# Measures, loads, residuals and spare steps of a two-layer attention and scan kernel put at other places in a hand-written order

## The chip, the cores and the metric

The kernel runs on one core of one Trainium2 chip. The metric is device time in microseconds (us). Three runs of the kernel before took 2679.15 to 2679.93 us, with a median of 2679.76.

## The reference

Two layers work on an image batch x of 2 × 56 × 56 tokens with 384 channels, in f32. Layer 0 is a neighborhood attention with 12 heads of 32 channels, in which each token sees 7 × 7 neighbors around it, and an MLP. Layer 1 is a projection, a depthwise convolution, four scans, and an MLP. Cut to what is computed:

```python
# layer 0
h   = layernorm(x) * ln1_g + ln1_b
q, k, v = split(h @ w_qkv + b_qkv)          # 12 heads of 32; q scaled by 32 ** -0.5
s   = q . k over the 7 x 7 neighbors + rpb  # window clipped at the edges
x   = x + (softmax(s) @ v) @ w_proj + b_proj
y   = layernorm(x) * ln2_g + ln2_b
x   = x + gelu(y @ w1 + b1) @ w2 + b2       # 384 -> 1536 -> 384
# layer 1
p     = (layernorm(x) * n1_g + n1_b) @ w_in + b_in      # 384 -> 768
local = depthwise_conv_3x3(p, k_conv)
scan(z): y[t] = 0.6 * y[t-1] + 0.4 * z[t]   # along rows and columns, both ways
mixed = 0.25 * (lr + rl + tb + bt) + local
x     = x + (layernorm(mixed) * on_g + on_b) @ w_out + b_out
x     = x + gelu((layernorm(x) * n2_g + n2_b) @ w1 + b1) @ w2 + b2
```

(The last line is the same MLP as in layer 0, with layer 1's own weights.)

## The kernel before

The order in which every engine works is written out by hand: the program is built under a manual schedule, and each engine takes its instructions in the order in which the Python code issues them. There are five engines: PE (matmuls and transposes), DVE (vector work), ACT (activations and scaling), POOL (a few small operations) and SP (whose queue issues the DMAs).

**Attention.** The 6272 tokens are cut into 14 groups n of 448 tokens (8 rows of 56; NG = 7 groups per image). A group has four windows of 112 query tokens, and the heads come in three head groups hg. So a group takes 12 steps, k = 0 to 11, and the whole loop has NU = 168 steps s = 12n + k and four more to drain. `Unit` is the work of one step, `Window` that of three steps. A step issues

- on PE the scores `sc` (L515) of step s, the values `o` (L556) of step s − 2, the sums of exponentials (L563), and one or two **fillers**: items of the list `ahead` (queries or keys, L386, and values, of later groups), a projection (L582) of a finished group, or transposes (L357) of the normalized tokens of group n + 3;
- on DVE `pts` (L530, scores plus bias), small steps of the softmax (`sum` L546 and L548, `turned` L482, `rec` L488, `good` L492, `rec_t` L498, `og` L500), the residual addition after a projection (`xr`, L590), and the statistics of the layer norm of group n + 3, one token tile at a time (`measure_x`, which issues the statistics L214 and L215; behind the last tile come `rs` L219, a power on POOL L222, and `sh` L233);
- on ACT the exponential of `pts` (L536), the normalization of `xg` (L240, `normalize_x`) and the copies out of PSUM;
- on POOL the softmax totals (L484, L494), and the addition of a bias to a residual tile (`add_bias`, L576), four steps after that tile was asked for.

SP's queue takes stores (L642) at the start of a step, then residual loads (L571, `load_residual`), group loads of `xg` (L302), bias loads (L316), and the vt load of a window (L465, values back from DRAM, in which `v_d` holds them). `ahead` has 9 items in odd groups and 10 in even ones. The tuple `spare` lists the steps k that take no item of `ahead`. In groups 0 to 11 these are (3, 4, 5) in odd groups and (4, 6) in even ones. Projections of the group before are issued from k = 3 on. From END = 12 on (the last two groups) there is little left in `ahead`, and projections go to the steps in THEN.

During the last 16 steps of the loop the two weights of layer 0's MLP are loaded in six parts (`w_parts`, L625), and behind the last step the first groups of the next stage (`xs`, tag "xa", L609) and four residual tiles.

```python
        if s < NU and hg == 2 and s + 1 < NU:
            ws[i + 1] = Window(i + 1)
        if s >= NU - UG - 4 and hg == 2 and w_parts:
            w_parts.pop(0)()
```

**The passes.** Layer 0's MLP and layer 1's projection `w_in` follow, over groups of token tiles (128 tokens each; up to four tiles a group). Then layer 0's MLP goes on beside the convolution and the scans of layer 1 (`Beside`, with the jobs `Band` and `Columns`, mostly on DVE): these are issued between PE's groups as their due times come, and `beside.until(...)` issues them up to a named job. `Columns` number NI = 6 jobs per image, one for every 128 channels, and store the mixed result to `mix_d` (L1259).

**The last stage** goes over the groups again: `load_mix` (L1274) loads a group's `mx` from `mix_d`, `measure` turns its tiles by PE (`xi`, L1288) and takes their statistics, `project_out` multiplies by `w_out`, and the MLP follows (`hid` L1080 and L1089, `y` L1096, out store L1526). `measure_beside` puts the measures of the next group between the twelve hidden columns m of the MLP of this group. The group `half_way` is the first that reaches into the second image, so it needs the last of that image's `Columns`; it is loaded tile by tile, 128 tokens of all channels at a time:

```python
            if g + 2 == half_way:
                beside.until((1, NI - 1))
                ahead = load_mix(g + 2)
```

Groups after `half_way` turn their tiles on DVE (L1299, `measure_by_vector`). The last DVE row, L1556, is the addition behind the last token tile.

Of the kernel before, what the change touches and what calls it, by code (L numbers as in the profile page):

```python
# [41 lines left out]
NH, KS, HD = 12, 7, 32  # L42
# [131 lines left out]
def block_kernel(ctx: ExitStack, tc: tile.TileContext, ins: dict, out: bass.AP):  # L174
# [467 lines left out]
            nc.sync.dma_start(out=dst, in_=src)  # L642


    tps = [any_bank() for c in range(NC)]
    halves = [Norm(sm) for h in range(2)]
    for h, norm in enumerate(halves):
# [39 lines left out]
        channels_of(2, c, any_bank)()  # L687
    load_bias(0, 3)
    for t in range(3):
        load_residual(t)  # L690
    shift_by_values(ep, ps_t, wproj, shift)
    sctx.close()

# [13 lines left out]
    for s in range(NU + 4):  # L707
        n, k, hg, i = s // UG, s % UG, s % NC, s // NC
        if s == NU:

            kctx.close()
            xp = ctx.enter_context(tc.tile_pool(name="x", bufs=2, side="right", reuse_waits="tile"))
            tail_pool = actx.enter_context(tc.tile_pool(name="a_tail", bufs=1))
            xs = {g: load_group(x1f, groups[g], "xa") for g in range(2)}
            for t in range(T2 // P - 4, T2 // P):
                load_residual(t, tail_pool, 4, 2)
        store_all()
        while load:
            load_residual(load.pop(0))
        if k == 0 and n < ng:  # L720
            vals = []
            if n + 1 < ng:
                ahead += [lambda n=n, m=m: query_or_key(n + 1, m, one_bank) for m in range(NC)]
                vals += tiles_of(n + 1)[2:]
            if n + 2 < ng:
                vals += tiles_of(n + 2)[:2]
            ahead += [lambda t=t: value(t, one_bank) for t in vals]
            if n + 2 < ng:
                ahead += [
                    lambda n=n, m=m: query_or_key(n + 2, m, one_bank) for m in range(NC, 2 * NC)  # L730
                ]

            spare = (3, 4, 5) if len(ahead) == 9 else (4, 6)

        if k == 2 and n + 4 < ng:
            load_x(n + 4)
        if k == 1 and n < ng:
            load_bias(n, NWC - 1)
        if n + 1 < ng and k in (4, 10):
            load_bias(n + 1, 0 if k == 4 else 1)  # L740
        if s == NU - UG - 4:
            ectx.close()
            wm = ctx.enter_context(tc.tile_pool(name="w_mlp", bufs=1, side="right"))
            w1, w2, w_parts = weights(0)
        if s < NU and hg == 2 and s + 1 < NU:
            ws[i + 1] = Window(i + 1)
        if s >= NU - UG - 4 and hg == 2 and w_parts:
            w_parts.pop(0)()

        if s <= NU:  # L750
            for take in taking:
                take()
            taking = []
        if s == NU + 1:
            sctx.close()
            ps_s = sctx.enter_context(tc.tile_pool(name="a_pss", bufs=4, space=PSUM))
        if s < NU:

            if s not in units:
                units[s] = Unit(ws[i], hg)  # L760
                units[s].scores()
                behind = Unit(ws[(s + 1) // NC], (s + 1) % NC) if s + 1 < NU else None
                if behind is not None and (units[s].m + behind.m) * TT <= BANK:
                    behind.scores(units[s].m)
                    units[s + 1] = behind
        new, before, last = units.get(s), units.get(s - 1), units.pop(s - 2, None)
        done = last.w if last is not None and last.hg == NC - 1 else None
        if last is not None:
            last.values()
        behind = ws.get(i - 1 - (hg == 0))  # L770
        if behind is not None and hg == 2:
            behind.invert()
        if behind is not None and hg == 0:
            behind.divide()
            if behind.j == NWC - 1:
                to_project += tiles_of(behind.n)
            ws.pop(behind.i)
        if n + 3 < ng and k < NT:
            measure_x(n + 3, k)
        for half in range(2):  # L780
            if new is not None:
                new.biased(half)
                new.numerators(half)
            if half == 0 and done is not None:
                done.take()
        if before is not None:
            before.gathered()
        if done is not None:
            done.gather()
        if n < END:  # L790
            if ahead and k not in spare:
                taking.append(ahead.pop(0)())
            if to_project and n < END - 1:
                taking.append(project(to_project.pop(0), turning_bank))
        elif ahead:
            if k != 3:
                taking.append(ahead.pop(0)())
        elif s - END * UG in THEN:
            taking.append(project(to_project.pop(0), one_bank))
        elif s > NU and s < NU + 4 and to_project:  # L800
            taking.append(project(to_project.pop(0), any_bank))
        for t in list(loaded):
            loaded[t] -= 1
            if loaded[t] < 0:
                add_bias(t)
        if n + 3 < ng:
            if k in (4, 5):
                for q in range(2 * k - 8, 2 * k - 6):
                    normalize_x(n + 3, q)
            if k in (8, 9, 11):  # L810
                taking.append(channels_of(n + 3, (8, 9, 11).index(k), turning_bank))
# [159 lines left out]
    def passes(xs, xn, w1, w2, between=lambda ps: None):  # L971
# [294 lines left out]
        def load_mix(g):  # L1266
            t0, n = dgroups[g]
            mx = io.tile([P, NI, MT], F32, name="mx")

            step = P if g == half_way else n * P  # L1270
            for t in range(0, n * P, step):
                for b, at, here, size in images(t0 + t, step):
                    here += t
                    nc.sync.dma_start(  # L1274
                        out=mx[:, :, here : here + size],
                        in_=mix_d[b][:, :, at : at + size].rearrange("m p t -> p m t"),
                    )
            x = load_group(x2_d, dgroups[g], "xa")
            if g >= half_way:
                add_row(x, dgroups[g][1], "b_out")  # L1280
            return mx, x, Norm(sm)
# [23 lines left out]
        def measure_beside(m, g, ahead):  # L1305


            n = dgroups[g][1]
            if g > half_way:
                if m % 2 == 0 and m // 2 < n:  # L1310
                    measure_by_vector(ahead[0], ahead[2], m // 2)
            elif m % 2 == 1 and 0 < m // 2 <= n:
                measure(ahead[0], ahead[2], m // 2 - 1)
            if m == 10:
                ahead[2].close(n)

        def project_out(g, mx, x, inner):
# [174 lines left out]
        for g, (t0, n) in enumerate(dgroups):  # L1492
# [37 lines left out]
                    add_row(x3, dgroups[g + 1][1], "b2_1")  # L1530
                beside.go(ROW_D)
            if g + 2 == half_way:
                beside.until((1, NI - 1))
                ahead = load_mix(g + 2)
        pctx.close()

# [90 lines left out]
```

## Time and profile before

| what | value |
|---|---|
| median of 3 runs | 2679.76 us (2679.15 to 2679.93) |
| profiled execution, own time | 2680.04 us |
| its span | 2678.2 us |
| PE busy | 2640.3 us (99%), 14963 instructions |
| DVE busy | 1963.2 us (73%), 3539 instructions |
| ACT busy | 898.7 us (34%) |
| POOL busy | 249.7 us (9%) |
| DMA | 298.99 MB moved, mean 112 GB/s |
| granted clock of PE, mean | 0.996 of full |

The span is the time from the first to the last recorded instruction; the execution's own time is the device time of that same run, 1.8 us more. Busy time is the time in which an engine has an instruction at work; PE's weight loads are counted on their own and lie beside its matmuls. The clock is what the throttle granted to PE: 1.00 is full rate and 0.50 half. The views used below are the table of waits (for every instruction and what released it: total us, times, longest), the windows (for a stretch of time: its length, the busy time of every engine, and the clock) and the timeline (instructions in order of time: start, duration, engine, line, operation, output and inputs).

### The profile page before, as it was taken

What the parts mean: (1) busy time and instruction counts of PE and PEld (TensorE: products, weight loads), DVE (VectorE), ACT (ScalarE), POOL (GpSimd) and SP (SyncE); (2) the same over time, 40 slices, a digit from 0 to 9 for tenths busy, and PEclk for the clock granted to TensorE, in tenths of its full rate; (3) what the DMA queues carried; (4) which work ended last, traced back from release to release, by engine and by line L of the source; (5) the groups of instructions that cost most, each with busy time, mean ns of one, the idle gap of its engine ahead of it and who ended that gap; (6) DMA issues with size and microseconds to landing.
All of it is one profiled execution on the core that took longest, in us unless ns stands there. A gap on an engine that the chain in (4) does not pass through costs nothing. (4 is left out here: it accounts for less than half of the span.)

```text
span 2678.2 us, 37275 instructions
## 1 busy us (share of the span) xinstructions
PE 2640.3 (99%) x14963; PEld 1473.9 (55%) x14963; DVE 1963.2 (73%) x3539; ACT 898.7 (34%) x1447; POOL 249.7 (9%) x264
## 2 busy tenths in 40 slices
PE   8999999999899999999999999999999899999999
PEld 4666666656655455555555555555555455555556
DVE  3778877876365698688989889888988627677652
ACT  4555555554322332223344422311143211111111
POOL 1111111111211100000010000000010011101100
PEclk9999999999999999999999999999999999999999
DMA  6323454224411132233346544533346401111000
GB/s 216 134 89 102 154 170 146 80 77 158 156 37 38 65 107 88 89 128 105 123 156 230 184 149 150 178 120 114 118 182 228 152 19 37 45 44 39 30 12 17
DMA packets 134249, 298.99 MB, mean 112 GB/s; under 512 B 11463, under 2 KB 89905, under 8 KB 131761
## 3 DMA queue, kind: packets, MB, share of 16 engines
q1 hardware_dynamic: 134064, 296.50, 32.3%
q8 instruction: 119, 1.95, 0.3%
q14 instruction: 66, 0.53, 0.1%
HBM read 180.86 MB, written 115.61 MB: 111 GB/s over the span
## 5 line engine op out<-in xcount | busy, mean ns | idle before, releaser
L1080 PE MATMUL mm<-hT,w 128*128 128x512 f32 (+2 forms) x1872 | 771.1, 569 | 0.4 <-ACT hT L254 0.2
L1080 PEld LDWEIGHTS mm<-hT,w 128*128 128x128 f32 x1872 | 352.7, 190 | 383.5 <-issue 352.1
L1089 ACT ACTIVATE hid<-mm,chan 128x512 f32<-128x512 f32 (+2 forms) x312 | 206.1, 661 | 683.3 <-PE mm L1080 683.2
L1096 PE MATMUL y_end<-w,hid 128*128 128x384 f32 x1200 | 395.2, 486 | 0.0
L1174 DVE SCALAR_TENSOR_TENSOR loc<-pt,taps,loc 128x990 f32<-128x990 f32 (+9 forms) x336 | 377.1, 1122 | 10.0 <-ACT loc L1156 1.7
L1096 PE MATMUL y<-w,hid 128*128 128x384 f32 x1152 | 379.4, 486 | 0.0
L1096 PEld LDWEIGHTS y_end<-w,hid 128*128 128x128 f32 x1200 | 227.5, 190 | 157.2
L1096 PEld LDWEIGHTS y<-w,hid 128*128 128x128 f32 x1152 | 218.2, 190 | 150.5 <-issue 1.0
L530 DVE TENSOR_TENSOR pts<-sc,bias 119x448 f32<-119x448 f32 (+3 forms) x336 | 220.9, 699 | 78.2 <-PE sc L515 75.2
L536 ACT ACTIVATE pts<-pts 119x448 f32<-119x448 f32 (+3 forms) x336 | 206.8, 642 | 191.3 <-DVE pts L530 187.9
L222 POOL TENSOR_TENSOR rs<-rs,mhalf 128x4 f32<-128x4 f32 (+4 forms) x67 | 87.1, 1300 | 1727.0 <-DVE rs L219 1691.6
L386 PE MATMUL ps<-hT,wqkv 128*128 128x448 f32 x504 | 212.0, 559 | 2.0 <-ACT qT L396 0.7
L1064 DVE STREAM_TRANSPOSE hT<-xn 32x96 f32<-32x96 f32 x672 | 181.1, 269 | 31.4 <-PE mm L1080 11.8
L1080 PE MATMUL mm<-hT,w_in 128*128 128x512 f32 (+2 forms) x468 | 191.9, 568 | 0.6 <-ACT hT L254 0.6
L240 ACT ACTIVATE xn<-xc,sh,rs 128x384 f32<-128x384 f32 x98 | 64.7, 698 | 268.6 <-DVE sh L233 268.5
L1080 PEld LDWEIGHTS mm<-hT,w_in 128*128 128x128 f32 x468 | 88.5, 190 | 102.1 <-issue 90.6
L386 PEld LDWEIGHTS ps<-hT,wqkv 128*128 128x128 f32 x504 | 90.2, 191 | 82.8 <-issue 73.1
L515 PEld LDWEIGHTS sc<-qT,kT 32*100 32x100 f32 (+3 forms) x3168 | 91.6, 170 | 67.1 <-issue 17.9
L1299 DVE STREAM_TRANSPOSE turned<-mx 32x192 f32<-32x192 f32 x336 | 123.3, 367 | 4.2
L515 PE MATMUL sc<-qT,kT 32*100 32x112 f32 (+3 forms) x3168 | 114.7, 272 | 6.5 <-DVE pts L530 5.8
L556 PE MATMUL o<-pts,vt 100*32 100x112 f32 (+3 forms) x3168 | 112.7, 266 | 3.8 <-DMA vt<-v_d 2.7
L582 PE MATMUL ps<-wproj,og 128*128 128x384 f32 x294 | 107.1, 503 | 3.6 <-DVE xr L590 3.6
(104 smaller groups left out, 2644.9 us busy)
## 6 DMA issues: line engine op xcount, KB each, us to landing
bias<-in_bias_t SPq DMA_DIRECT2D x16, 1344.0 KB
loc<-loc_d SPq DMA_DIRECT2D x24, 784.0 KB
mixed<-mix_d SPq DMA_DIRECT2D x24, 784.0 KB
mix_d<-mixed SPq DMA_DIRECT2D x24, 784.0 KB
xa<-x_d SPq DMA_DIRECT2D x22, 768.0 KB
p_d<-mx SPq DMA_DIRECT2D x10, 1536.0 KB
mx<-mix_d SPq DMA_DIRECT2D x10, 1536.0 KB
pt<-p_d SPq DMA_DIRECT2D x18, 560.0 KB
```

The costliest lines, as they stand in the source:

```text
L386: nc.tensor.matmul(ps, lhsT=wqkv[:, c, m * P : (m + 1) * P], rhs=hT[:, c, half_of(n)], start=c == 0, stop=c == NC - 1,)
L515: nc.tensor.matmul(sc[i // 2][: w.keys, i % 2, (first + c) * TT : (first + c + 1) * TT], lhsT=kT[d, hg, w.keys_at + r * w.kc : w.keys_at + ...
L530: nc.vector.tensor_tensor(self.of(half), sc[half][:n, :, at].rearrange("p h (c q) -> p h c q", q=TT), self.w.bias[:n, 4 * self.hg + h : 4 ...
L536: nc.scalar.activation(self.of(half), self.of(half), AF.Exp)
L556: nc.tensor.matmul(o[i * HD : (i + 1) * HD, hg, :], lhsT=w.vt[:n, c, h * HD : (h + 1) * HD], rhs=self.pts[:n, i, c, :], start=c == 0, stop ...
L582: nc.tensor.matmul(ps, lhsT=ogs[t // 7][:, c, at : at + P], rhs=wproj[:, c, :], start=c == 0, stop=c == NC - 1,)
L1064: nc.vector.transpose(hT[j : j + HD, :, k * P + i : k * P + i + HD], xn[i : i + HD, k, :].rearrange("p (c q) -> p c q", c=NC)[:, :, j : j ...
L1080: nc.tensor.matmul(ps[:, : n * P], lhsT=w[:, c, m * P : (m + 1) * P], rhs=hT[:, c, : n * P], start=c == 0, stop=c == NC - 1,)
L1089: nc.scalar.activation(t[:, : n * P], ps[:, : n * P], AF.Gelu, bias=col(b1, m))
L1096: nc.tensor.matmul(ps, lhsT=t[:, k * P : (k + 1) * P], rhs=w[:, m, :], start=m == 0, stop=m == len(lhs) - 1,)
L1174: nc.vector.scalar_tensor_tensor(to, pt[:, lo + dy - self.top : hi + dy - self.top, xt : xt + n], self.tap(dy, dx), to, ALU.mult, ALU.add,)
L1299: nc.vector.transpose(t[j : j + HD].rearrange("p (m c) -> p m c", m=NI)[:, :, i : i + HD], mx[i : i + HD, :, k * P + j : k * P + j + HD],)
```

## The change

The change adds no arithmetic to the result, and it touches seven places:

1. Twelve matmuls of two constant tiles are issued to PE ahead of everything else, into a bank that is overwritten later.
2. The first three residual tiles get their bias on POOL eight steps after they were asked for instead of four.
3. In the attention loop `measure_x` of group n + 3 is issued at k = 2 to 5 instead of 0 to 3, and `normalize_x` at k = 6 and 7 instead of 4 and 5.
4. In group 11 (n == END − 1) the steps without an item of `ahead` are 3, 6 and 9 instead of 3, 4 and 5.
5. A window's values are asked for at hg == 1 of the window before instead of hg == 2, through the whole loop, and the weights of the MLP, also at hg == 1, two parts at a time.
6. At attention's end the four residual tiles and the two group loads are issued as two tiles, a group, two tiles, a group, instead of two groups and then four tiles.
7. At the turn to `half_way`, `load_mix` loads channels instead of tiles: five of the six channel blocks after `until((1, NI - 2))`, the sixth after `until((1, NI - 1))`. The measures of that group come two hidden columns later, and its norm closes at m = 11 instead of 10.

```diff
@@ -642,6 +642,10 @@
             nc.sync.dma_start(out=dst, in_=src)
 
 
+
+    warm = any_bank()
+    for _ in range(12):
+        nc.tensor.matmul(warm[:HD, :P], lhsT=ones_hd, rhs=ident, start=True, stop=True)
     tps = [any_bank() for c in range(NC)]
     halves = [Norm(sm) for h in range(2)]
     for h, norm in enumerate(halves):
@@ -687,7 +691,7 @@
         channels_of(2, c, any_bank)()
     load_bias(0, 3)
     for t in range(3):
-        load_residual(t)
+        load_residual(t, steps=8)
     shift_by_values(ep, ps_t, wproj, shift)
     sctx.close()
 
@@ -711,9 +715,11 @@
             kctx.close()
             xp = ctx.enter_context(tc.tile_pool(name="x", bufs=2, side="right", reuse_waits="tile"))
             tail_pool = actx.enter_context(tc.tile_pool(name="a_tail", bufs=1))
-            xs = {g: load_group(x1f, groups[g], "xa") for g in range(2)}
-            for t in range(T2 // P - 4, T2 // P):
-                load_residual(t, tail_pool, 4, 2)
+            xs = {}
+            for g in range(2):
+                for t in range(T2 // P - 4 + 2 * g, T2 // P - 2 + 2 * g):
+                    load_residual(t, tail_pool, 4, 2)
+                xs[g] = load_group(x1f, groups[g], "xa")
         store_all()
         while load:
             load_residual(load.pop(0))
@@ -731,6 +737,8 @@
                 ]
 
             spare = (3, 4, 5) if len(ahead) == 9 else (4, 6)
+            if n == END - 1:
+                spare = (3, 6, 9)
 
         if k == 2 and n + 4 < ng:
             load_x(n + 4)
@@ -742,10 +750,12 @@
             ectx.close()
             wm = ctx.enter_context(tc.tile_pool(name="w_mlp", bufs=1, side="right"))
             w1, w2, w_parts = weights(0)
-        if s < NU and hg == 2 and s + 1 < NU:
+        if s < NU and hg == 1 and s + 2 < NU:
             ws[i + 1] = Window(i + 1)
-        if s >= NU - UG - 4 and hg == 2 and w_parts:
-            w_parts.pop(0)()
+        if s >= NU - UG - 4 and hg == 1:
+            for part in w_parts[:2]:
+                part()
+            del w_parts[:2]
 
         if s <= NU:
             for take in taking:
@@ -775,8 +785,8 @@
             if behind.j == NWC - 1:
                 to_project += tiles_of(behind.n)
             ws.pop(behind.i)
-        if n + 3 < ng and k < NT:
-            measure_x(n + 3, k)
+        if n + 3 < ng and 2 <= k < 2 + NT:
+            measure_x(n + 3, k - 2)
         for half in range(2):
             if new is not None:
                 new.biased(half)
@@ -804,8 +814,8 @@
             if loaded[t] < 0:
                 add_bias(t)
         if n + 3 < ng:
-            if k in (4, 5):
-                for q in range(2 * k - 8, 2 * k - 6):
+            if k in (6, 7):
+                for q in range(2 * k - 12, 2 * k - 10):
                     normalize_x(n + 3, q)
             if k in (8, 9, 11):
                 taking.append(channels_of(n + 3, (8, 9, 11).index(k), turning_bank))
@@ -1267,14 +1277,21 @@
             t0, n = dgroups[g]
             mx = io.tile([P, NI, MT], F32, name="mx")
 
-            step = P if g == half_way else n * P
-            for t in range(0, n * P, step):
-                for b, at, here, size in images(t0 + t, step):
-                    here += t
+            def load_channels(lo, hi):
+                for b, at, here, size in images(t0, n * P):
                     nc.sync.dma_start(
-                        out=mx[:, :, here : here + size],
-                        in_=mix_d[b][:, :, at : at + size].rearrange("m p t -> p m t"),
+                        out=mx[:, lo:hi, here : here + size],
+                        in_=mix_d[b][lo:hi, :, at : at + size].rearrange("m p t -> p m t"),
                     )
+
+            if g == half_way:
+
+                beside.until((1, NI - 2))
+                load_channels(0, NI - 1)
+                beside.until((1, NI - 1))
+                load_channels(NI - 1, NI)
+            else:
+                load_channels(0, NI)
             x = load_group(x2_d, dgroups[g], "xa")
             if g >= half_way:
                 add_row(x, dgroups[g][1], "b_out")
@@ -1309,9 +1326,12 @@
             if g > half_way:
                 if m % 2 == 0 and m // 2 < n:
                     measure_by_vector(ahead[0], ahead[2], m // 2)
-            elif m % 2 == 1 and 0 < m // 2 <= n:
-                measure(ahead[0], ahead[2], m // 2 - 1)
-            if m == 10:
+            else:
+                late = 2 if g == half_way else 0
+                k = (m - late) // 2 - 1
+                if m % 2 == 1 and 0 <= k < n:
+                    measure(ahead[0], ahead[2], k)
+            if m == (NHID - 1 if g == half_way else 10):
                 ahead[2].close(n)
 
         def project_out(g, mx, x, inner):
@@ -1530,7 +1550,6 @@
                     add_row(x3, dgroups[g + 1][1], "b2_1")
                 beside.go(ROW_D)
             if g + 2 == half_way:
-                beside.until((1, NI - 1))
                 ahead = load_mix(g + 2)
         pctx.close()
```

## The prediction

> **What bounds the kernel now.** I read the page first: PE is busy 2640.3 of 2678.2 us, so every arithmetic step is already under it, and a change can win only the 37.9 us in which PE stands still, plus the time in which PE is busy at half clock. The waits of PE say where it stands still:
>
> ```profile
> PE xi L1288 <- DMA mx<-mix_d: 7.7, 1, 7.7
> PE ps L357 <- DVE xg L226: 7.0, 1, 7.0
> PE sc L515 <- DVE pts L530: 5.8, 10, 1.3
> PE ps L582 <- DVE xr L590: 3.6, 2, 2.6
> PE o L556 <- DMA vt<-v_d: 2.7, 2, 2.4
> ```
>
> Columns: total us, times, longest. The reader is to see that few places carry nearly all of it. I located each in windows of 1 or 2 us: the start (0 to 7), attention's first group (61 to 70), its last three groups (576 to 706), and the turn of the last stage (2124.9 to 2132.5). Between 100 and 550 us PE idles 0.02 us in 50. Then the granted clock:
>
> ```profile
> 584.00:590.00 6.00, 6.00 (x49) 3.46 (x42) 4.26 (x7) 1.68 (x3) 0.00 (x0) 0.50 0.00 0
> ...
> 652.15:655.56 3.41, 1.97 (x60) 1.54 (x56) 2.28 (x5) 1.04 (x2) 0.00 (x0) 1.00 0.68 223
> ...
> 202.90:206.70 3.80, 3.80 (x65) 2.44 (x64) 3.73 (x10) 2.77 (x5) 0.71 (x2) 1.00 0.49 150
> ```
>
> After the length come PE, PEld, DVE, ACT, POOL busy; the third number from the end is PEclk. First line: PE fully busy, at half clock[...]. Second: a stretch with PE at 1.97 of 3.41 us; right after it the clock is 0.5 to 659.0. Third, the line that decides most: in the middle of an ordinary group PE is full, and DVE is at 3.73 of 3.80 us. There DVE has no slack. The order of time there:
>
> ```profile
> 196.19 0.16 DVE L219 SCALAR_TENSOR_TENSOR rs<-mv,ones 112x4 f32<-112x4 f32 x1
> 197.55 0.16 DVE L233 SCALAR_TENSOR_TENSOR sh<-mv,rs 112x4 f32<-112x4 f32 x1 [1.20 <-POOL rs L222]
> 197.63 1.61 DVE L530 TENSOR_TENSOR pts<-sc,bias 100x672 f32<-100x672 f32 x2
> ...
> 203.91 0.31 DVE L492 SCALAR_TENSOR_TENSOR good<-totals,good 128x11 f32<-128x11 f32 x2
> 204.14 1.61 DVE L530 TENSOR_TENSOR pts<-sc,bias 100x672 f32<-100x672 f32 x2
> ```
>
> The close of a norm (rs, POOL's power, sh) holds DVE 1.20 us, at step k=3 of group 3; next sc starts at 199.24, just when its bank is free. At k=5 pts starts at 204.14, next sc at 206.69.
>
> [...] the slow stretches here (583.9 to 590.7, 655.6 to 659.0, 679.4 to 682.8, 2130.1 to 2136.9) are one or two times 3.4 us and lie on one grid[...]. [...] transposes from 7.02, yet full rate only at 13.9. [...] two `good` take 1.75 us while POOL adds residuals at 63.56 to 66.46, else 0.31. [...] in SP's order near attention's end:
>
> ```profile
> 661.44 0.41 SPq L642 DMA_DIRECT2D x_d<-xr  x1
> 670.78 0.33 SPq L571 DMA_DIRECT2D xr<-in_x  x1
> 671.16 1.51 SPq L465 DMA_DIRECT2D vt<-v_d  x2
> 672.71 0.47 SPq L625 DMA_DIRECT2D w<-in_L_conv_w  x1
> ```
>
> The reload of xr waits 9 us for its store to land behind bias and weights; the values queue behind it.
>
> **The change part by part** (negative is faster).
>
> 1. Twelve warm matmuls at the start. An L386 matmul of 448 columns takes 0.75 us cold, so one of 128 columns about 0.21, twelve 2.6 us, from 1.6 (ones_hd) to 4.2: ahead of 7.02, so they cost nothing. Gain: at most the half rate from 9.96 to 13.89 (2.0 us) plus some 0.5 of the transposes. [...] No row shows such a case. Bounds 0 and −2.5; I take −0.5.
>
> 2. First group: the three residual adds on POOL (2.90 us) move from step 4 to 8 and no longer hold `good` (1.44 us gained on DVE); the norm close arrives at the same place. By hand pts of k=5 starts at 66.13 instead of 65.45. Taken +0.5, bounds −1 and +1.
>
> 3. Measures move from k=0..3 to k=2..5, normalizing from k=4,5 to 6,7, in groups 0 to 10. Nothing is added, but from k=4 on DVE must do two stats (0.69 each) and the close, into the full stretch. Group 3: k=3 is released from its wait and pts starts at 196.5, when sc is there; then xr 199.40, stats, pts of k=4 200.56 (0.40 later than now), rec and good to 204.54, stats begin; from stats to pts is 2.25 us (145.38 to 147.63 in group 2): pts of k=5 at 206.79, against 204.14. Sc sees the banks 0.91 and 1.67 us after a pts starts (575.48 to 576.39 and 577.15), and its last 20 matmuls take 0.82: it ends at 209.28 instead of 207.52, +1.75. The next sc waits another 0.2. So interior odd groups (1, 3, 5, 9): 4 × 1.95 = 7.8. Group 7 (pts of 448, 1.15 us): 0.9. Even groups have two fillers of 2.2 us at k=5, which hide it, but 0.3 is left at k=6: four interior ones, 1.2. Queued behind the waiting sh are pts, exp on ACT, and PE's sc. ACT is at 2.28 of 3.80 at k=6, so 1.29 of normalizing fits. Sum +9.9. Below: 0, if PE were ahead somewhere; above: +20, with the clock (rival B).
>
> 4. Group 11: free steps 3, 4, 5 become 3, 6, 9. Now PE starves 2.6 us at 576 to 584 and then runs 6.8 us at half clock (3.4 lost). Separate free steps leave about 0.56 (0.23 + 0.33, as at 576 to 577) and 0.3: −1.8; the halving goes[...]: −3.4. One separate step may still stall later: +0.3. Sum −4.9, bounds −6 and −1.5.
>
> 5. Values a step sooner, weights in three pairs instead of six single parts. Six DMAs of 768 KB move: of SP's queue each issue is 0.46 us, no matter. SP's order still puts values behind the reload of xr; a pair behind the bias adds 0.79 MB at some 300 GB/s, 2.6 us, to the landing of x_d, so vt of the third window may come 1.5 us later, and its landing was 5.6 us after issue with one weight part behind it. On the other side two stalls (2.7) and one slow stretch (1.7) may go. In the steady groups the earlier load waits on SP for a v_d store just issued (about 2.2 us), with four steps in hand: hidden. Bounds −4.4 and +4; taken 0.
>
> 6. Tail: no weight stands ahead of the residuals (0.46 + 1.31 us of SP, 1.6 MB), and two residuals go before each group load. Now xr of tile 44 is asked for at 700.53 and PE waits 1.0 + 2.6 for adds. By hand: x_d of tile 41 goes out at 690.5 instead of 694.06, lands at 694.5; xr lands at 697, POOL 1.0, add 698.3; PE wants its bank at 701. First group (xa) lands by 692 instead of 695.9, so the adds behind the norm come in time. −3.6, bounds −3.9 and −1.5. The 0.7 wait before the first transposes stays.
>
> 7. Turn of the last stage. Five of six channels are loaded ahead of the last stores, when DMA stands idle (2110 to 2116 and on); only the last channel (256 KB) remains behind them. First use moves two hidden columns later: due at 2124.86 + 2 × 1.28 = 2127.4, its last transpose at 2128.1. The store lands at 2126.55 as now, the load's data follow the second store (to 2127.9), landing 2129.2 to 2130.8. Left to wait: 1.1 to 2.7, say 1.9 instead of 7.67; no halving, which cost 2.2 (4.4 us at half from 2132.5). Sum −8.0, bounds −9.9 and −5. The last measure now ends behind the twelfth column: rs is ready some 2.4 us after the last transpose, while the first two token groups take 3.8 us of PE: hidden, 0.9 us to spare.
>
> Sum: −0.5 + 0.5 + 9.9 − 4.9 + 0 − 3.6 − 8.0 = **−6.6 us**, against the profiled execution (2680.04; 1.8 us around its span). The median of the runs lies 0.3 below that: 2679.8 − 6.6 = 2673.1.
>
> **Rivals.** A: DVE's wait at k=5 is absorbed, so step 3 costs 0. For it: PE idles nowhere in these groups today. Against it: DVE 3.73 of 3.80 just there. Then −16.5: 2663. B, slower: the stall of step 3 halves the clock. Between two full-array fillers lie then some 3.4 us of small matmuls with 1.5 idle, much like the second window line above. Each halving of 3.4 us costs 1.7, of 6.8 us 3.4. [...] Slower than now from two groups at 3.4 (6.8 against 6.6); with all four 13.6 − 6.6 = +7: 2687. C: the paired weights make the values late, step 5 at +4: 2677, no change that counts. That the warm matmuls do nothing for the clock is inside step 1.
>
> **How the numbers follow.** 0.2% is 5.4 us, about what a measurement of this kernel tells from no change. Likeliest, steps as summed: 0.51, own range 2667 to 2679, of it 0.34 faster, 0.16 same, 0.01 slower. A 0.22, all faster. C 0.12: 0.02 faster, 0.10 same. B 0.15, slower. Together 0.58, 0.26, 0.16. The range takes in A's side and part of B: 2661 to 2682.
>
> **What would show it.** Step 3: new waits of sc on pts of about 1 us in groups 1, 3, 5, 9, and PE at some 48 of 50 us there; none means A. Step 7: xi's wait near 2 us and clock 1.0 after. Step 4: no clock of 0.5 near 584. Step 6: the 2.6 wait of L582 gone. Step 5: vt's wait at 676 shows its sign. Clock below 1.0 between 100 and 550 us means B. The forecast is wrong if the odd groups keep their length, or if the turn still waits over 5 us.

## The result: 8 us slower, and the profile after

The changed kernel takes 2687.9 us (median of 12 runs, 2685.16 to 2690.35), the kernel before 2679.85 in the runs beside it: a ratio of 1.0029 with a 95% interval of 1.0021 to 1.0036. The prediction was 2673.1, with a range of 2661 to 2682: wrong in sign. The profiled execution has a span of 2685.3 us and an own time of 2687.20, against 2678.2 and 2680.04.

First the waits of PE in the changed kernel (total us, times, longest):

```profile
PE sc L515 <- DVE pts L530: 9.5, 16, 1.3
PE o L556 <- DMA vt<-v_d: 5.0, 4, 2.6
PE ps L424 <- ACT vs L431: 4.3, 10, 0.6
PE o L556 <- ACT pts L536: 2.3, 1, 2.3
...
PE ps L357 <- DVE xg L226: 1.5, 2, 1.3
```

The 7.7 us of `xi` are gone, and so are the 3.6 us of projections waiting for `xr`. In their place scores wait more often for `pts` (16 times instead of 10), values wait for vt longer, and a wait that the kernel before does not have stands ten times: values matmuls (L424) behind ACT's copy of earlier values (L431).

The same stretch of an ordinary odd group that the prediction showed, now at 209.2, one of the last group's waits, and the turn of the last stage (length, then PE, PEld, DVE, ACT and POOL busy; the third number from the end is the clock):

```profile
209.21:213.41 4.20, 3.30 (x48) 1.93 (x42) 2.90 (x11) 0.10 (x1) 1.73 (x3) 1.00 0.29 89
691.50:694.50 3.00, 0.45 (x12) 0.24 (x16) 2.68 (x6) 1.05 (x2) 0.67 (x2) 1.00 0.85 281
2133.00:2145.00 12.00, 12.00 (x29) 5.32 (x28) 8.56 (x9) 2.75 (x4) 0.00 (x0) 1.00 0.69 242
```

PE stands still for 0.9 us in a group that ran without a gap before; in the second line it works 0.45 of 3 us while DMA moves 281 GB/s; in the third it never stops and keeps its full clock.

To see where the 7.07 us of span come from, take the start of the same DVE row (`pts`, L530, at each group's first step; the additions behind MLP and `project_out` later) in both traces and subtract. All columns are us of a stretch against the kernel before:

| kernel | to group 0 | group 0 | groups 1–10 | group 11 | attention's end | passes | turn | behind it | span |
|---|---|---|---|---|---|---|---|---|---|
| before (length) | 47.58 | 41.83 | 473.75 | 46.55 | 123.96 | 1337.12 | 169.96 | 437.50 | 2678.24 |
| after | +0.87 | +0.72 | +17.28 | −3.89 | +2.60 | +0.35 | −10.02 | −0.82 | +7.07 |

Attention's end runs from group 12 to the first output of the MLP. Group 11, the turn and the last column agree to 0.2 us in every kernel below that has these parts of the change. The start and attention's end scatter. Fifteen profiles have the same twelve matmuls at the start, and their first column lies between −0.4 and +4.9. What parts them is the clock: in seven of them (e1, e4, e6, e7, g3, g4 and h2 below) it is 0.50 for 3.4 or 6.8 us from about 26 us on, and these lie at +1.7 to +4.9; the other eight lie at −0.4 to +1.2 (f3, where it falls for 3.4 us at 10 us already, at +0.9). Runs of one kernel differ by some 4 us, which would fit, but with one profile of each kernel that is not shown.

### The profile page after: what moved, and what is told of

It is laid out like the page before. It is cut to its first block, busy times and chain, and to the rows that moved or that the text cites. A ratio compares the mean times of both kernels' runs of the same rounds, so it can differ in the third digit from the quotient of the medians.

```text
span 2685.3 us, 37352 instructions
## 1 busy us (share of the span) xinstructions
PE 2646.1 (99%) x14987; PEld 1478.3 (55%) x14987; DVE 1967.6 (73%) x3539; ACT 897.6 (33%) x1447; POOL 250.0 (9%) x264
## 5 line engine op out<-in xcount | busy, mean ns | idle before, releaser
L1184 DVE SCALAR_TENSOR_TENSOR loc<-pt,taps,loc 128x990 f32<-128x990 f32 (+9 forms) x336 | 377.1, 1122 | 10.3 <-ACT loc L1166 1.7
L530 DVE TENSOR_TENSOR pts<-sc,bias 119x448 f32<-119x448 f32 (+3 forms) x336 | 220.8, 699 | 93.8 <-PE sc L515 91.9
L386 PE MATMUL ps<-hT,wqkv 128*128 128x448 f32 x504 | 210.2, 555 | 3.6 <-ACT vs L431 1.5
L386 PEld LDWEIGHTS ps<-hT,wqkv 128*128 128x128 f32 x504 | 89.4, 189 | 83.3 <-issue 71.6
L424 PE MATMUL ps<-wqkv,hT 128*128 128x384 f32 x294 | 106.9, 502 | 4.3 <-ACT vs L431 4.3
```

The lines of the kernel that those rows point to most:

```text
L386: nc.tensor.matmul(ps, lhsT=wqkv[:, c, m * P : (m + 1) * P], rhs=hT[:, c, half_of(n)], start=c == 0, stop=c == NC - 1,)
L424: nc.tensor.matmul(ps, lhsT=hT[:, c, at : at + P], rhs=wqkv[:, c, 2 * C :], start=c == 0, stop=c == NC - 1,)
L530: nc.vector.tensor_tensor(self.of(half), sc[half][:n, :, at].rearrange("p h (c q) -> p h c q", q=TT), self.w.bias[:n, 4 * self.hg + h : 4 ...
L1184: nc.vector.scalar_tensor_tensor(to, pt[:, lo + dy - self.top : hi + dy - self.top, xt : xt + n], self.tap(dy, dx), to, ALU.mult, ALU.add,)
```

## The experiments

Medians are set beside that of the kernel before in the same runs (2679.7 to 2680.7).

### Who makes the ordinary groups longer

The measures alone taken back, put into the kernel before alone, and the normalization alone moved:

```diff
 e1_measures_back (from after)
-        if n + 3 < ng and 2 <= k < 2 + NT:
-            measure_x(n + 3, k - 2)
+        if n + 3 < ng and k < NT:
+            measure_x(n + 3, k)
...
-            if k in (6, 7):
-                for q in range(2 * k - 12, 2 * k - 10):
+            if k in (4, 5):
+                for q in range(2 * k - 8, 2 * k - 6):
 e2_measures_alone (from before): both hunks the other way round
 e3_normalize_alone (from before): the second hunk the other way round
```

> The changed kernel with the measures at k = 0 to 3 and the normalization at k = 4 and 5 again; all else as changed. Theory D (the moved measures cost all that the trace shows between the start of group 0 and the start of group 11, that is 18.0 us, less some 0.7 that the first group loses to its late bias): 2688 - 17.3 = 2670.6. Rival (they cost what was predicted, 9.9 us, and the rest comes of the values asked for a step sooner in every window): 2678. In the trace under D: no wait of sc or of a values matmul (L424) between 100 and 550 us.

> The kernel before with the move of measures (k = 2 to 5) and normalization (k = 6, 7) alone. Theory D: 2680 + 17.3 = 2697, and groups 1 to 10 each longer by 2.8 (odd) and 1.3 (even) as in the changed kernel. Rival (part of the growth needs the other edits): about 2690. If group 11 starves as before, its clock of 0.5 stays.

> The kernel before with only the normalization moved to k = 6 and 7; the measures stay at k = 0 to 3. It divides the cost between DVE (measures beside full steps) and ACT (four normalizations ahead of the copy of values that a bank waits for). Theory D-ACT (the waits of L424 for the copy L431, 4.3 us in ten groups, are ACT's own and need no late measures): 2680 + 4 = 2684. Rival (ACT is only late because sh comes late from DVE): 2680, no wait of L424.

Measured: 2668.64, 2701.51 and 2680.92 us (ratios 0.9958 [0.9944, 0.9971], 1.0075 [1.0061, 1.0088], 1.0005 [0.9997, 1.0013]). In e1 groups 1 to 10 have the length of before to 0.01 us; in e2 they are 18.61 us longer, with nothing else of the change there; in e3 1.37. So the move costs 2687.9 − 2668.64 = 19.3 us, all of it its own, and theory D holds, with 2 to 4 us more than it reckoned. In e2 nearly all of the rest (21.6 in all) lies in group 0 (+2.9), where in this kernel alone the clock fell for 3.4 us. D-ACT falls: moving ACT's part alone costs 1.4, not 4.

One long window over the steady groups shows it, first the changed kernel, then e1:

```profile
100.00:550.00 450.00, 439.96 (x5911) 268.37 (x5910) 345.97 (x715) 235.26 (x432) 63.65 (x112) 1.00 0.36 117
```

```profile
100.00:550.00 450.00, 449.85 (x6161) 276.01 (x6161) 359.45 (x742) 246.23 (x448) 67.58 (x118) 1.00 0.37 121
```

PE idles 10 us against 0.15 (10.5 in groups 1 to 10 as a whole), yet these groups lost 17. The missing 7 us are inside busy rows, as PE's order of time in group 3 of the changed kernel shows:

```profile
208.51 0.83 PE L515 MATMUL sc<-qT,kT 32*100 32x112 f32 x24
...
213.27 0.44 PE L515 MATMUL sc<-qT,kT 32*100 32x112 f32 x4 [0.90 <-DVE pts L530]
214.04 0.82 PE L515 MATMUL sc<-qT,kT 32*100 32x112 f32 x20 [0.33 <-DVE pts L530]
...
217.83 1.22 PE L515 MATMUL sc<-qT,kT 32*100 32x112 f32 x24
...
220.58 0.59 PE L424 MATMUL ps<-wqkv,hT 128*128 128x384 f32 x1 [0.63 <-ACT vs L431]
```

Ordinarily the 24 matmuls of a step take 0.83 us (first line). Behind the late banks (the places of `sc` that DVE must have read before PE may write them again) they take 1.6 with a gap in between, and in the next step 1.22 with no gap shown at all; why their rows grow is not shown. An idle sum alone would have explained 60% of the loss. The order of DVE in the same place is the one worked out in the prediction:

```profile
210.12 0.55 DVE L214 BATCH_NORM_STATS2 st<-xg 112x6 f32<-112x384 f32 x1
210.71 0.18 DVE L215 BATCH_NORM_AGGREGATE mv<-st 112x2 f32<-112x6 f32 x1
210.93 0.16 DVE L219 SCALAR_TENSOR_TENSOR rs<-mv,ones 112x4 f32<-112x4 f32 x1
212.29 0.16 DVE L233 SCALAR_TENSOR_TENSOR sh<-mv,rs 112x4 f32<-112x4 f32 x1 [1.20 <-POOL rs L222]
212.37 1.62 DVE L530 TENSOR_TENSOR pts<-sc,bias 100x672 f32<-100x672 f32 x2
```

From `stats` to `pts` 2.25 us, and the first four scores start 0.9 us later at 213.27. What the prediction lacked is on ACT:

```profile
217.50 1.47 ACT L536 ACTIVATE pts<-pts 100x672 f32<-100x672 f32 x2 [2.72 <-DVE pts L530]
218.88 1.29 ACT L240 ACTIVATE xg<-xg,sh,rs 112x384 f32<-112x384 f32 x2
220.07 0.46 ACT L431 COPY vs<-ps 128x384 f32<-128x384 f32 x1
```

The copy that frees the bank of the next values stands behind two normalizations (1.29 us), which the change put at k = 6, and these behind an exponential that waits for the late `pts`. In e3, where `pts` is on time, the same wait is at most 0.3 us.

Three more kernels vary DVE's load around that place: a filler on PE there, less work on DVE, and a move by one step only.

```diff
 f3_filler_at_5 (from after)
-            spare = (3, 4, 5) if len(ahead) == 9 else (4, 6)
+            spare = (3, 4, 6) if len(ahead) == 9 else (4, 6)
 g3_late_no_guard (from after)
-            for edge, inside in ((SUM_MAX, ALU.is_le), (1.0 / SUM_MAX, ALU.is_ge)):
-                nc.vector.scalar_tensor_tensor(good, self.totals, edge, good, inside, ALU.mult)
 g4_one_step_late (from after)
-        if n + 3 < ng and 2 <= k < 2 + NT:
-            measure_x(n + 3, k - 2)
+        if n + 3 < ng and 1 <= k < 1 + NT:
+            measure_x(n + 3, k - 1)
...
-            if k in (6, 7):
-                for q in range(2 * k - 12, 2 * k - 10):
+            if k in (5, 6):
+                for q in range(2 * k - 10, 2 * k - 8):
```

> The changed kernel (late measures, pairs, all else) with the free steps of odd groups at 3, 4 and 6 instead of 3, 4 and 5, so that a filler of 2.2 us stands on PE in step 5. Theory D (DVE, full at k = 5, hands its banks back late once, and a filler covers it as in even groups): odd groups grow by about 1.3 instead of 2.76, 2688 - 6 = 2682. Rival (DVE stays behind for the rest of the group, or ACT's copies set the time): 2688 or more.

> The changed kernel (late measures) without the update of the guard that tells whether a softmax sum is in range: two small DVE instructions (L492, 0.31 us together) fewer in every third step, k = 5 among them, so that part of the computation is left out. Theory D (pts of k = 5 is late by DVE's own work, microsecond for microsecond): each of groups 1 to 10 shorter by some 0.3, 2688 - 3 = 2685, and every wait of sc in step 5 shorter by 0.3. Rival (the latency of POOL's power in the norm's close, not DVE's work, sets it): those waits unchanged, 2688.

> The changed kernel with the measures at k = 1 to 4 and normalization at 5 and 6: one step later than before instead of two. In odd groups the windows of k = 3 to 8 have three pieces (pts 672 wide, 1.61 us, and two sums) and those of k = 0 to 2 two pieces (448, 1.12 us). Theory D (the cost is what the measures put into the wide steps: one statistic less than at 2 to 5): odd groups grow by 2.76 - 0.7 = 2.1 at most, 1.3 at least; the whole 2688 - 3 to 7 = 2681 to 2685. Rival (only the close at k = 5 hurts, since there the softmax inverse lies too): under 2675.

Measured: 2692.78 (1.0046 [1.0032, 1.0061]), 2685.57 (1.0015 [1.0008, 1.0021]) and 2683.93 us (1.0014 [1.0007, 1.0021]). Groups 1 to 10 are 22.67, 14.79 and 15.86 us longer than before.

The filler did not do what D expected of it. It moved the wait from k = 5 to k = 6 and made it longer (group 3 of f3):

```profile
215.21 0.83 PE L515 MATMUL sc<-qT,kT 32*100 32x112 f32 x24
...
218.44 0.44 PE L515 MATMUL sc<-qT,kT 32*100 32x112 f32 x4 [1.49 <-DVE pts L530]
219.20 0.82 PE L515 MATMUL sc<-qT,kT 32*100 32x112 f32 x20 [0.33 <-DVE pts L530]
```

So the lateness is no single blow at k = 5: DVE has no slack in the following steps either (busy 5.90 of 6.00 us from 214 to 220 in the changed kernel), and PE meets it at the first step without a filler. Group 3 is 2.07 us longer than before here instead of 2.77 (ACT's 0.70 is gone), but groups 1, 5, 7 and 9 are 3.5 to 5.0 longer (single groups are taken from the first scores of each on PE). There the clock falls to 0.50, as in group 1, where the two windows are neighbors:

```profile
116.00:119.38 3.38, 1.82 (x52) 1.53 (x56) 3.35 (x6) 2.11 (x4) 0.00 (x0) 1.00 0.41 133
119.38:122.79 3.41, 3.41 (x21) 1.87 (x10) 3.08 (x7) 3.35 (x6) 0.19 (x1) 0.50 0.39 126
```

This is the prediction's rival B. The length of the wait alone does not decide it: group 3, shown above with 1.49 us, kept its clock, and so did every group of the changed kernel, whose clock reads 1.00 from the span's start to 670.4 us; but with waits of 0.9 us, as in the changed kernel, one group each of e2 and of e4 below lost it.

The guard gave back what it takes: in group 3 the first wait of scores is 0.62 us instead of 0.90, groups 1 to 10 are 2.5 us shorter, 0.28 in most groups for a pair of instructions of 0.31. The wait behind POOL's power is the same in both kernels, so DVE's own work in front of `pts` counts nearly microsecond for microsecond. The 1.20 us in which DVE waits for POOL stand in front of the same `pts`, and no run takes them away. One step earlier (g4) odd groups grow by 2.1 and even ones by 1.2, near the upper end that D gave. Both kernels still lose most of what the change loses; only the old place is free. There, at k = 0 to 2, the windows have two pieces (`pts` 448 wide and one sum) and DVE idles 2.11 us ahead of one `pts` in the kernel before; at k = 3 to 8 they have three (672, and two sums), and DVE has next to nothing left (0.07 of 3.80 us in group 3 of the kernel before). Groups 6 and 7 have two pieces at every step: there the change costs 0.26 and 1.46 us, where groups 8 and 9 lose 1.33 and 2.76.

### Who makes attention's end longer

Values and weights as before, with late and with early measures, and each half alone:

```diff
 e4_values_weights_back (from after); e5_measures_values_weights_back (the same from e1)
-        if s < NU and hg == 1 and s + 2 < NU:
+        if s < NU and hg == 2 and s + 1 < NU:
             ws[i + 1] = Window(i + 1)
-        if s >= NU - UG - 4 and hg == 1:
-            for part in w_parts[:2]:
-                part()
-            del w_parts[:2]
+        if s >= NU - UG - 4 and hg == 2 and w_parts:
+            w_parts.pop(0)()
 e6_weights_single (from e1): the second hunk alone
 e7_values_back (from e1): the first hunk alone
```

> The changed kernel with the values' load at hg == 2 and the weights one part at a time again; the measures stay late. Theory C (pairs of weights sit ahead of a residual's store, the reload of that residual holds SP, and the values behind it come late): the waits of o at attention's end fall from 5.0 to about 2.7 us, the half clock with them, 2688 - 4.5 = 2683.5. Rival (the loss at the end comes of the order of residuals and groups behind step NU): 2688, waits as in the changed kernel.

> The changed kernel with early measures again, and the values' load and the weights as before (hg == 2, one part at a time). What is left of the change are the matmuls at the start, the later bias of three residuals, group 11's free steps, the residuals ahead of the groups at attention's end, and the turn of the last stage. From 2668.6 (early measures alone): theory C gives back what the values and weights cost at the end, 4 to 6 us by the stretch from group 13 to the first MLP output (+2.6 in the changed kernel, -3.4 without): 2664. Rival (that stretch only scatters from run to run): 2668.5.

> Early measures, the values a step sooner as changed, but the weights one part at a time at hg == 2. Tells the two halves of that edit apart. If the pairs are the cost (C): as with both taken back, 2664. If the earlier values are (they come ahead of other loads and wait for a store just issued): 2668.5.

> Early measures, the weights in pairs as changed, but the values asked for at hg == 2 as before. If the pairs are the cost (C): 2668.5 or more, up to 2671, since values come later still behind the pairs. If the earlier values are: 2664.

Measured: 2684.34 (1.0013 [1.0007, 1.002]), 2661.45 (0.9938 [0.9925, 0.9952]), 2660.75 (0.9931 [0.9918, 0.9945]) and 2668.31 us (0.9956 [0.9943, 0.997]). The pairs of weights are the cost: 3.6 us with late measures (2687.9 − 2684.34), 7.2 and 7.9 with early ones (e1 against e5 and e6). The earlier values are worth nothing either way (e5 against e6, e1 against e7: under 1 us).

Why the pairs cost: SP's order in the changed kernel.

```profile
676.98 1.03 SPq L625 DMA_DIRECT2D w<-in_L_conv_w  x2
678.11 1.10 SPq L642 DMA_DIRECT2D x_d<-xr  x1
688.28 0.34 SPq L571 DMA_DIRECT2D xr<-in_x  x1
688.72 1.50 SPq L465 DMA_DIRECT2D vt<-v_d  x2
```

The store of a residual goes out behind a pair of weights at 678.1; the reload into that buffer waits for it until 688.3, and the values stand behind the reload. Two kernels test that: the reload behind the values of its own step, and more buffers, so that it need not wait.

```diff
 e8_reload_last (from e1)
-        while load:
+        while load and s < NU - UG - 4:
             load_residual(load.pop(0))
...
             del w_parts[:2]
+        while load:
+            load_residual(load.pop(0))
 f1_reload_buffers (from e1); f2_single_buffers (the same from e6)
-    def load_residual(t, pool=lp, bufs=3, steps=4):
+    def load_residual(t, pool=lp, bufs=5, steps=4):
```

> Early measures, values sooner and weights in pairs as changed, but from the step on where the weights begin (s = NU - UG - 4) the reload of a residual is issued behind the values and weights of that step instead of ahead of them. Theory Q (the reload waits on SP for its store to land, some 10 us behind the weights, and the values behind it on the queue are late for that alone): the waits of o for vt fall from 5 us to under 1.5, 2663. Rival (values and weights share the DMA engines, so the values are late whatever stands ahead of them): waits of 3 to 5 us stay, 2668.

> As with early measures alone taken back (values sooner, weights in pairs), but with five buffers for the residual tiles in attention instead of three, so that a reload need not wait for the store of the tile three before it. Order on every engine and on SP is the same. The run with the reload behind the step's own values left the question open: the reload of a step without values stood ahead of the next values all the same. Theory Q (SP is held by the reload that waits for its store, and that store lands behind the pair of weights): the waits for vt fall from 8.0 us to under 2, 2661 or less. Rival (DMA is shared): waits of over 4 us stay, 2667.

> Early measures, values sooner, weights one part at a time, and five residual buffers. Theory Q: with nothing that holds SP the values' earlier place takes effect too, vt's waits under 1 us and one slow stretch less: 2657 to 2659. Rival: as with single weights alone, 2661.

Measured: 2666.09 (0.995 [0.9936, 0.9964]), 2656.79 (0.9915 [0.9903, 0.9928]) and 2657.37 us (0.9915 [0.9902, 0.9928]). e8 told little: vt's waits stayed at 7.6 us, because a reload of a step without values still stood ahead of the next values. f1 decides. SP's longest wait in the changed kernel, ahead of it:

```profile
SPq L571 <- DMA x_d<-xr: 40.1, 7, 9.3
```

In f1 no reload waits for a store any more, and SP's order at the same place has no hole:

```profile
653.35 0.34 SPq L642 DMA_DIRECT2D x_d<-xr  x1
653.73 1.10 SPq L571 DMA_DIRECT2D xr<-in_x  x1
654.93 1.56 SPq L465 DMA_DIRECT2D vt<-v_d  x2
656.54 2.55 SPq L625 DMA_DIRECT2D w<-in_L_conv_w  x2
```

All waits for vt are gone, with the same pairs of weights and the same bytes. Attention's end is 8.8 us shorter than before (e1: 2.6 longer), and its clock stays at 1.00 to the end of the span (mean of the profiled run: 1.0; e1: 0.997). So theory Q holds, and the sharing of DMA, the rival, makes no values late in f1. f1 has the lowest median of this study, 0.85% below the kernel before; with single weights (f2) the time is the same. So a pair costs 7.9 us with three buffers (e1 against e6) and nothing that shows with five (f1 against f2).

The sum of SP's waits does not tell these kernels apart: the reloads wait 38.4 us in the kernel before, 40.7 in e1 and 38.6 in e6. The clock does. At attention's end it is 0.50 for 13.7 us in the changed kernel and in e1, for 6.8 in the kernel before and in e6, for 3.4 in e4 and e5, and never in f1. Six values matmuls (L424) take 4.21 us at 0.50 (586.15, in the kernel before) and 2.20 at 1.00, so PE loses nearly half of such time; between the changed kernel and e4 (10.3 us less of it) that is an estimated 4.9 us of the 6.0 by which attention's end differs in their profiles. Why a pair turns a few late values into so many slow stretches stays open.

The order of residuals and groups, at three places:

```diff
 h1_after_groups_first (from after); h2_values_weights_back_groups_first (from e5); g2_best_groups_first (from f1)
-            xs = {}
-            for g in range(2):
-                for t in range(T2 // P - 4 + 2 * g, T2 // P - 2 + 2 * g):
-                    load_residual(t, tail_pool, 4, 2)
-                xs[g] = load_group(x1f, groups[g], "xa")
+            xs = {g: load_group(x1f, groups[g], "xa") for g in range(2)}
+            for t in range(T2 // P - 4, T2 // P):
+                load_residual(t, tail_pool, 4, 2)
```

> The changed kernel with the two group loads ahead of the four residuals again. With five buffers that order made no difference at attention's end; here the reloads hold SP as in the changed kernel. As predicted (the order saves two waits for residuals, 3.6 us): 2691.5, with waits of L582 for xr. Rival (the residuals land in time because no weights stand ahead of them any more, so the order is worth nothing): 2688, no such wait.

> Early measures, values and weights as before, and the groups ahead of the residuals too: attention's end stands in the order of the kernel before, but for group 11. If the order saves 3.6 us where the sixth weight stands ahead of the residuals: 2661.5 + 3.6 = 2665. Rival (its waits for residuals were 3.6 us there all the same, so the order only shifts them): 2661.5 within 1.5.

> The fastest version with the two group loads ahead of the four residuals again at attention's end, as before the change. It prices that edit alone. As predicted (two waits of projections for residuals, 3.6 us, come back): 2660. Rival (with nothing holding SP the residuals land in time either way): 2657.

Measured: 2687.27 (1.0026 [1.002, 1.0033]), 2663.97 (0.9936 [0.9922, 0.995]) and 2658.17 us (0.9918 [0.9905, 0.9932]), so −0.6, +2.5 and +1.4 beside the kernels that they come from. In g2 the way from step 8 of the last group to the MLP's first output is as long as in f1 to 0.01 us; the difference lies in the start (1.6 us) and in one slow stretch ahead of that step (1.6), where the two kernels are the same. In h1, with the old order, no projection waits for `xr`. In e5 and h2 both do; their lines:

```profile
PE ps L582 <- DVE xr L590: 3.6, 2, 2.4
```

```profile
PE ps L582 <- DVE xr L590: 4.2, 2, 2.8
```

The waits stay with the new order where the sixth weight is issued late, and go with the old order where the weights are through: it was the weights' place, not the residuals', that freed them. Whether the 2.5 us of h2 hold a part of the order's own is open; it is within what that stretch and the start scatter (h2's start alone is 3.2 us longer than e5's).

### The start

```diff
 f4_no_warm (from e5); g1_best_no_warm (from f1)
-    warm = any_bank()
-    for _ in range(12):
-        nc.tensor.matmul(warm[:HD, :P], lhsT=ones_hd, rhs=ident, start=True, stop=True)
```

> The version with early measures, values and weights as before, without the twelve matmuls at the start. Theory S (the landing of group 1's tokens at 15 to 17 us and DMA's full load set the end of the start, so that a faster clock ends in a wait there): no difference, 2661.5 within 1.5. Rival (the full clock from 5 us on is worth the 1.9 us that the matmuls gain): 2663.5.

> The fastest version so far (early measures, values sooner, weights in pairs, five residual buffers), without the twelve matmuls at the start. Its end of attention is calm, so that the start shows alone. Theory W (the matmuls are worth the cold rate of the first projections, 1.9 us, and more where group 1's tokens land late): 2656.8 + 2 to 5 = 2659 to 2662. Theory S (they end in a wait): 2656.8 within 1.5.

Measured: 2666.32 (0.9944 [0.9931, 0.9957]) and 2657.73 us (0.9911 [0.9896, 0.9926]). f4 is 4.9 above e5. In the profiles 2.7 us of the difference lie in the start and 4.2 at attention's end, which the matmuls don't touch; why the end differs is not shown. g1, whose end is calmer, is only 0.9 above f1, and the runs of f1 themselves lie between 2654.4 and 2661.4. Here is f1's start:

```profile
9.59 7.03 PE L386 MATMUL ps<-hT,wqkv 128*128 128x448 f32 x18 [0.62 <-ACT hT L362]
...
25.20 5.15 PE L386 MATMUL ps<-hT,wqkv 128*128 128x448 f32 x13 [1.49 <-ACT vs L431]
```

The clock column reads 1.00 from the span's start in both traces of the pair, but the matmuls' own times change: in the changed kernel the rows of the twelve (L648) take 0.42 us each up to about 5 us and 0.27 from then on; in the kernel before those of L386 take 0.95 at the median up to 13.8 and 0.54 behind it. So the first 18 projections take 7.03 us instead of 8.94, in f1 as well. But PE then waits 1.49 us for a copy at 25 us, which it did not before, and at about 26 us stand the slow stretches that seven of the fifteen profiles with the matmuls have; of the five profiles without the matmuls only e3's has one, at 28 us. So of the 1.9 us won 1.5 end in a wait, and what is left, between nothing and 5 us, these runs do not settle.

## Why the prediction was wrong, step by step

All numbers are of the profiled pair (sum −6.6 predicted, +7.07 measured), or of the runs where named.

- **Step 3, measures (+9.9): the term that failed.** Measured +17.28 in groups 1 to 10; with group 0, which the prediction has in step 2, the move costs 19.3. The mechanism was right, and at the place worked out to the size: scores of step 5 in group 3 come 1.72 us later (predicted 1.75), those of the next step another 0.38 (0.2). Missing were ACT's copy behind the normalizations (0.70 in that group, 0.38 in group 2; ten waits, 4.3 us), and the even groups, where for "two fillers of 2.2 us at k=5, which hide it, but 0.3 is left at k=6" 0.95 us were left in group 2, at k = 6 and 7. "ACT is at 2.28 of 3.80 at k=6, so 1.29 of normalizing fits" counted busy time and not what stands behind it in the queue. By kind: odd groups 12.5 for 8.7, even ones 4.8 for 1.2. The +20 given as the bound was nearly met.
- **Steps 5 and 6, attention's end (0 and −3.6): +2.6 together.** Rival C's mechanism is what happened, at +3.6 to +7.9 instead of its +4, and its chain (a pair of weights, a store, a reload, the values) was named in the step and then taken at 0. It reckoned that one slow stretch might go; instead the time at half clock doubled, from 6.8 to 13.7 us. Step 6 gave its effect to the wrong cause: the waits for `xr` left, but because the weights were through.
- **Step 7, the turn (−8.0): −10.0.** PE does not wait at all. "Say 1.9" of waiting was too careful; everything else, the slow stretch included, was as written.
- **Step 4, group 11 (−4.9): −3.9.** The slow stretch went (−3.4), but the waits did not: PE is idle for 2.6 us of that group in both kernels, where the prediction reckoned 1.8 less.
- **Step 2, group 0 (+0.5): +0.72.** The hand-made schedule holds: it put `pts` of k=5 at 66.13, and it stands at 67.26 behind a start that is 0.87 later. With the additions on POOL later, `good` takes 0.31 us instead of 1.75, and the group alone gets 1.26 shorter by it, as in every kernel with early measures; the measures take 1.98 of it back.
- **Step 1 (−0.5): not settled.** The pair f1 and g1 says −0.9, e5 and f4 −4.9; the profiled pair has +0.87, which lies within the scatter of the start.
- **The rest:** +0.35 in the passes, −0.82 behind the turn, of which no row of work is the cause: the last output is issued 2.75 us before the span's end instead of 3.57. The cause stays open. The sum of the prediction, 2679.8 − 6.6, is 2673.2 and not 2673.1.

Rival B named 2687 and the time is 2687.9, but for another reason: no ordinary group of the changed kernel lost its clock. It did so in f3 in four groups, and in one group each in e2 (group 9) and e4 (group 5), where it cost 0.6 us.

The waits of the reloads on SP carried more than the prediction made of them: they are 40.1 us in the changed kernel and 40.7 in e1, and without them the kernel is 11.9 us faster (e1 against f1).

## What to carry to other kernels

Before side work is moved, list for each step how much slack the engine has with the shapes of that step: the measures were free at k = 0 to 3, where three of the four lie beside windows of two pieces, and cost 17 us at k = 2 to 5, where three of them lie beside windows of three. Count what stands behind a moved instruction in its own queue, not only whether its busy time fits. And where a load waits for a store, ask first for another buffer: two more tiles here were worth 11.9 us with the weights in pairs and 3.4 with single ones, and behind them the order of the weights and of the last loads made no difference that these runs show.

## What the hardware did that was not expected

- PE's loss hides in busy rows: 24 score matmuls take 0.83 us in a row, and 1.22 to 1.41 in the steps around a late bank, with hardly a gap between them; idle rows showed 10 of 17 us.
- A stretch of 3.38 us with PE 1.82 busy at full clock was followed by 3.41 us at half (f3), while 3.30 busy of 4.20 in the changed kernel left the clock alone. Group 3 of f3, with the same wait of 1.49 us, left it alone too.
